# Eight places instead of five for layer 1's normalized rows, the neighbour weights moved to a later pool, and the first x tiles issued ahead of the convolution taps

## The chip, the cores and the metric

The kernel runs on one core of one Trainium2 chip. The metric is the device time of one execution in microseconds, and of several runs the median is compared. The engines are TensorE (PE in the profile; its weight loads are PEld), VectorE (DVE), ScalarE (ACT), GpSimd (POOL) and SyncE (SP), which here only issues DMAs.

## What is computed

The input x has 128 graphs of 128 nodes with 256 channels, and adj holds one 128x128 adjacency matrix for each graph. Two layers follow one another, each of them with a normalization in front and a residual around it:

```
h = relu(layernorm(x));  x = x + layer0(h, adj)
h = relu(layernorm(x));  x = x + layer1(h, adj)

layer0:  x_conv = relu(bn2(conv17(relu(bn1(conv1(h))))) + h)      # along the nodes
         s = h @ w_se.T + b_se;  A = exp(-|s_n - s_m|^2) * adj
         x_nmp = A @ relu(h @ w_msg.T + b_msg)
         result = GRU(input = [x_conv, x_nmp], state = h)
layer1:  the first 25 nodes, in five groups of 25, 9, 7, 6 and 6 of them:
         out_g = gcn(gcn(h_g, adj_g, W1[g], b1[g]), adj_g, W2[g], b2[g])
         fused = sum over g of softmax(fusion_w)[g] * out_g
```

All is in fp32. `gcn` normalizes the adjacency of its group by the degrees, multiplies by the weights and by the adjacency, and applies a ReLU.

## The kernel before

The 128 graphs form 32 groups of four (`q`), and the groups form two batches of 16 (`bat`). The convolution of width 17 is done through a small Fourier transform, so its weights are transformed once and then multiply the spectrum of the whole batch. For each batch there are two stages:

- `stage_a` (group by group): load x (`load_xa`, `load_x`, L362, on SP's queue, four tiles in its pool), layer normalization (`moments`, L271 to L274; `normalize`, L279), transposes with a ReLU (L389, L391), a store of the result to DRAM (`hTd`), the convolution of width 1 (L400, with `c1w`; L403, L405) and the forward transform (L411), which fills the spectrum `X`.
- `stage_b`: for each frequency, three products of the spectrum with the transformed taps (`wf`, loaded from the DRAM array `wfd`, L500), stored as `yd`.

Beside the first two stages runs a lane of other work: `tap_weights` (it transforms the taps, L453 and L458, and writes them to `wfd` through POOL's queue; in its middle it calls `load_late`), and then `early(q)` for each group, which loads `hT` and adj (L538, L540) and does the `neighbours` part: `pse` (L579), `ef` (L584, L587), the messages `pm` with `wmsg` (L599) and `msg` with `bmsg` (L602, L603), distances and adj (L611, L613), and the sum over neighbours (L624).

After both batches a last, long loop runs to the end of the program. In it are `stage_n` and `stage_c` for each group (the gates of the GRU: products at L706, gates at L719 to L807; then on POOL six operations for each group, L810 to L813; transposes back at L830, stores at L839) and layer 1:

- `setup_1` once;
- `rows(q)`: the layer normalization of the first 32 rows of each of a group's graphs: statistics (L904 to L906), a power on POOL (L907), then the normalized row `x1h` (L910 on VectorE, ReLU L911 on ScalarE);
- `prepare(blk)` for a block of four groups: degrees and normalized adjacency (L927 on POOL, L932 on VectorE, L938 and L943 on TensorE);
- `block(blk)`: products `py` of `x1h` with the adjacency (L989), copied into `yz` (L991, L992), two layers of weights (`first`, L1006 and L1008; `second`, L1015 and L1017), and the way back (L1037 to L1060), with the stores of the block on POOL's queue (L1069).

The order of the instructions is not the hardware's choice. Each stage is a Python generator, which yields the TensorE time that its step costs and the delay until its next step is due. The class `Order` keeps a clock of its own and picks, among lanes with weights, the step that is due and has had least of its share. Every engine then runs its own list in this order, and waits at an instruction until its operands are there and its place is free. So a delay in a `yield` and a condition in a `while` move instructions in the lists of all engines. `rows(q)` waits in this planner until `PY_DONE` holds row q − 5, since `x1h` has five places; block `blk` needs the rows 4·blk to 4·blk + 3, one for each group.

The start of the program issues, in this order: on ScalarE's queue the first constants and vectors; then the x tile of group 0 (SP), `c1w` (ScalarE), the x tile of group 1 (SP), the first taps `wt0` (five transfers, dealt to SP, POOL and ScalarE in turn) and the x tile of group 2 (SP). `fold()` then has the normalization of group 0 and the folding of the first batch norm into `c1w`.

## Time and profile before

| | |
|---|---|
| median of 9 runs | 2147.03 us (2141.74 to 2148.88) |
| profiled execution, its own time | 2141.94 us |
| its span, first to last instruction | 2140.1 us |
| granted clock of TensorE, mean | 0.983 |
| busy: TensorE, VectorE, ScalarE, POOL | 2071.3, 1152.7, 702.9, 719.3 us |
| bytes moved by DMA | 281.62 MB, mean 132 GB/s |

The stages lie in the span so: batch 0's `stage_a` until about 190 us and its `stage_b` from 206 to about 365; batch 1's until about 550 and 700; the last loop from there to 2140. Times in the span are counted from its start. In the lines of the profile the first number is the start, the second the busy time of what the line gathers, then come engine, line and operation, and in brackets the idle time of that engine just before, with what ended it.

### The profile page before, as it was taken

What the parts mean: (1) busy time and instruction counts of PE and PEld (TensorE: products, weight loads), DVE (VectorE), ACT (ScalarE), POOL (GpSimd) and SP (SyncE); (2) the same over time, 40 slices, a digit from 0 to 9 for tenths busy, and PEclk for the clock granted to TensorE, in tenths of its full rate; (3) what the DMA queues carried; (4) which work ended last, traced back from release to release, by engine and by line L of the source; (5) the groups of instructions that cost most, each with busy time, mean ns of one, the idle gap of its engine ahead of it and who ended that gap; (6) DMA issues with size and microseconds to landing.
All of it is one profiled execution on the core that took longest, in us unless ns stands there. A gap on an engine that the chain in (4) does not pass through costs nothing.

```text
span 2140.1 us, 30439 instructions
## 1 busy us (share of the span) xinstructions
PE 2071.3 (97%) x11124; PEld 1631.9 (76%) x11124; DVE 1152.7 (54%) x2711; ACT 702.9 (33%) x1545; POOL 719.3 (34%) x894
## 2 busy tenths in 40 slices
PE   6999999899999999999999999999999999999988
PEld 5667888788888777787678778868877787778765
DVE  5665444776444456545544554555555555644532
ACT  3564222344222243223223333233233323223223
POOL 2443665331565124303313233223223323232230
PEclk9999999999999999999999999999999999999999
DMA  8987878654787534222323223223232322323121
GB/s 180 277 259 238 274 261 263 190 168 138 242 260 255 164 94 139 73 77 72 87 60 111 66 80 101 71 77 81 83 89 69 94 89 72 83 73 101 36 67 50
DMA packets 186742, 281.62 MB, mean 132 GB/s; under 512 B 20637, under 2 KB 139938, under 8 KB 186594
## 3 DMA queue, kind: packets, MB, share of 16 engines
q1 hardware_dynamic: 155762, 184.81, 30.4%
q0 software_dynamic: 30000, 94.13, 13.7%
q8 instruction: 88, 1.44, 0.3%
q10 hardware_dynamic: 832, 0.74, 0.2%
q14 instruction: 60, 0.49, 0.1%
HBM read 187.34 MB, written 92.27 MB: 131 GB/s over the span
## 4 chain that ended last, share of the span: by engine, by line
PE 89%; DVE 3%; DMA 3%; POOL 2%; issue 1%; ACT 1%; SPq 0%; POOLq 0%; DVEq 0%; ACTq 0%
PE p L706 35%; PE pa L500 7%; PE pg L775 5%; PE ph L1006 5%; PE pz L1015 5%; PE pm L599 5%; PE pc L400 4%; PE pb L500 3%; PE pi L671 3%; PE pf L411 3%; PE px L624 3%; DMA wfd<-ws 2%; PE pg L1049 1%; PE po L830 1%; PE ph L389 1%
## 5 line engine op out<-in xcount | busy, mean ns | idle before, releaser
L810 POOL TENSOR_TENSOR d<-hTc,r 128x512 f32<-128x512 f32 x64 | 81.5, 1274 | 389.5 <-ACT r L807 389.4
L839 POOL DMA_DIRECT2D out<-xt x128 | 71.9, 567 | 250.0 <-DVE xt L836 245.7
L500 PE MATMUL pa<-wf,X 128*128 128x256 f32 x640 | 152.8, 382 | 0.0
L706 PE MATMUL p<-tc,wrz 128*128 128x256 f32 x512 | 132.3, 381 | 4.1 <-DVE tc L551 4.1
L706 PE MATMUL p<-th,wrz 128*128 128x256 f32 x512 | 132.6, 382 | 1.9 <-ACT u L737 1.9
L706 PE MATMUL p<-tm,wrz 128*128 128x256 f32 x512 | 132.3, 381 | 0.0
L500 PEld LDWEIGHTS pa<-wf,X 128*128 128x128 f32 x640 | 118.0, 190 | 17.2 <-issue 3.0
L523 DVE SCALAR_TENSOR_TENSOR y<-pa,kk 128x512 f32<-128x512 f32 x78 | 53.8, 690 | 140.5 <-ACT kk L522 140.3
L400 PE MATMUL pc<-c1w,hTa 128*128 128x256 f32 x512 | 124.7, 390 | 2.8 <-ACT ef L587 2.2
L719 ACT ACTIVATE r<-r,brz 128x256 f32<-128x256 f32 x128 | 58.1, 500 | 200.8 <-DVE r L752 172.9
L599 PE MATMUL pm<-wmsg,hT 128*128 128x256 f32 x512 | 122.3, 384 | 0.0
L775 PE MATMUL pg<-hTc,whn 128*128 128x512 f32 x256 | 120.9, 616 | 0.0
L1006 PE MATMUL ph<-yz,w 128*128 128x96 f32 (+3 forms) x640 | 114.4, 335 | 6.6 <-DVE yz L991 6.6
L1006 PEld LDWEIGHTS ph<-yz,w 128*128 128x128 f32 x640 | 92.0, 201 | 29.2 <-issue 16.5
L688 DVE SCALAR_TENSOR_TENSOR xc<-pc,s_bn,hTc 128x256 f32<-128x256 f32 x128 | 53.1, 477 | 110.6 <-PE pc L685 110.6
L400 PEld LDWEIGHTS pc<-c1w,hTa 128*128 128x128 f32 x512 | 96.2, 196 | 21.4 <-DVE h L403 4.0
L1008 ACT ACTIVATE hh<-ph,vec 128x96 f32<-128x96 f32 (+3 forms) x160 | 64.1, 402 | 147.4 <-PE ph L1006 138.3
L706 PEld LDWEIGHTS p<-tc,wrz 128*128 128x128 f32 x512 | 97.6, 191 | 18.2 <-DVE tc L551 4.9
L599 PEld LDWEIGHTS pm<-wmsg,hT 128*128 128x128 f32 x512 | 96.6, 191 | 15.3 <-issue 2.7
L706 PEld LDWEIGHTS p<-tm,wrz 128*128 128x128 f32 x512 | 97.9, 191 | 13.5
L1015 PE MATMUL pz<-hh,w 128*128 128x96 f32 (+3 forms) x640 | 107.5, 322 | 0.0
L706 PEld LDWEIGHTS p<-th,wrz 128*128 128x128 f32 x512 | 95.6, 191 | 14.1 <-ACT u L737 2.3
(197 smaller groups left out, 4470.1 us busy)
## 6 DMA issues: line engine op xcount, KB each, us to landing
wf<-wfd SPq DMA_DIRECT2D x160, 256.0 KB, 3.2
wfd<-ws POOLq DMA_DIRECT2D x64, 320.0 KB, 7.2
yd<-y POOLq DMA_DIRECT2D x80, 256.0 KB, 3.8
yt<-yd SPq DMA_DIRECT2D x64, 320.0 KB, 5.1
w<-in_W SPq DMA_DIRECT2D x40, 512.0 KB, 3.6
xa<-in_x SPq DMA_DIRECT2D x128, 128.0 KB, 4.9
hTd<-hTa POOLq DMA_DIRECT2D x32, 512.0 KB, 5.0
hT<-hTd SPq DMA_DIRECT2D x32, 512.0 KB, 4.5
```

What stands on the lines that cost most here:

```text
L400: nc.tensor.matmul(pc[:, i], hT[:, k, (2 * h + i) * N:(2 * h + i + 1) * N], c1w[:, k], start=(k == 0), stop=(k == 1))
L411: nc.tensor.matmul(pf[:, i, :F * NB], h1[:, 2 * h + i, k * P:(k + 1) * P], fwd, start=True, stop=True)
L500: nc.tensor.matmul(ps, xk(k), WF[f][:, k, s], start=(k == 0), stop=(k == 1))
L599: nc.tensor.matmul(pm[:, i], hT[:, k, j * N:(j + 1) * N], wmsg[:, k], start=(k == 0), stop=(k == 1))
L624: nc.tensor.matmul(px[:, dc, i], msgs[h][:, i, dc * P:(dc + 1) * P], aT[:, 2 * h + i], start=True, stop=True)
L671: nc.tensor.matmul(pi[b * 64:(b + 1) * 64], inv[:F], yt[:, b::2], start=True, stop=True)
L706: nc.tensor.matmul(ps[:, m], w[:, i, k, m * P:(m + 1) * P], factor(i, x, t), start=first and j == 0, stop=last and j == len(n) - 1)
L775: nc.tensor.matmul(pg, whn[:, k, dc * P:(dc + 1) * P], hT[:, k], start=(k == 0), stop=(k == 1))
L810: nc.gpsimd.tensor_sub(d, hT[:, dc], r[:, dc])
L839: nc.gpsimd.dma_start(out=out[q * GB + j, WIDE:].rearrange("(t n) c -> n t c", n=WIDE), in_=xt[j * WIDE:(j + 1) * WIDE, 1:4])
L1006: nc.tensor.matmul(ph, w1[:, k, m * P:(m + 1) * P], yz[:, k, :, o:o + n], start=(k == 0), stop=(k == 1))
L1015: nc.tensor.matmul(pz, w2[:, g, m, cc * P:(cc + 1) * P], hs[g][:, m], start=(m == 0), stop=(m == 3))
```

## The change

Four edits, each of a few lines:

1. `rows(q)` waits for `PY_DONE` of q − 8 in place of q − 5, `x1h` has eight places in place of five, and the delay between a row's statistics and its normalization is 4.0 in place of 2.5 in the planner's clock.
2. `wmsg` (2 KB of each partition) and `bmsg` (1 KB) are no longer tiles of the pools that live throughout; they are tiles of the pool `fr`, which is opened when `tap_weights` ends and closed when the neighbour part has been done for all groups. The three new places of `x1h` have 1 KB each.
3. So their loads (256 KB and 128 KB, on SP's queue) are issued at the end of `tap_weights`, after the pool is opened, and not in `load_late`.
4. At the start, `c1w` is issued on SP's queue after the x tiles of groups 0 and 1, and all five transfers of the first taps follow it on SP's queue; before, they were dealt to three queues.

In the changed file the lines from `load_late` up to the new loads stand four lines higher than before, and those from `stage_b` on where they stood or one or two lines further down.

```
-    wmsg = wp.tile([P, 2, D], FP, name="wmsg")
-    bmsg = cp.tile([P, D], FP, name="bmsg")
...
     def load_late():
         nc.sync.dma_start(out=wse, in_=w_se.rearrange("(k p) o -> p k o", p=P))
         nc.sync.dma_start(out=cst[:, CFIRST:], in_=consts[:, CFIRST:])
-        nc.sync.dma_start(out=wmsg, in_=w_msg.rearrange("(k p) o -> p k o", p=P))
-        nc.sync.dma_start(out=bmsg, in_=b_msg.partition_broadcast(P))
...
         LATE["fr"] = near.enter_context(tc.tile_pool(name="fr", bufs=1, reuse_waits="tile"))
+        LATE["wmsg"] = LATE["fr"].tile([P, 2, D], FP, name="wmsg")
+        LATE["bmsg"] = LATE["fr"].tile([P, D], FP, name="bmsg")
+        nc.sync.dma_start(out=LATE["wmsg"], in_=w_msg.rearrange("(k p) o -> p k o", p=P))
+        nc.sync.dma_start(out=LATE["bmsg"], in_=b_msg.partition_broadcast(P))
...
-                    nc.tensor.matmul(pm[:, i], hT[:, k, j * N:(j + 1) * N], wmsg[:, k],
+                    nc.tensor.matmul(pm[:, i], hT[:, k, j * N:(j + 1) * N], LATE["wmsg"][:, k],
...
-        while not (q in C_DONE and -1 in P_DONE and (q < 5 or q - 5 in PY_DONE)):
+        while not (q in C_DONE and -1 in P_DONE and (q < 8 or q - 8 in PY_DONE)):
...
-        yield 0.0, 2.5
-        x1h = S["x1h", q] = S["pool"].tile([P, D], FP, tag="x1h", name=f"x1h{q}", bufs=5)
+        yield 0.0, 4.0
+        x1h = S["x1h", q] = S["pool"].tile([P, D], FP, tag="x1h", name=f"x1h{q}", bufs=8)
...
     load_xa(0)
-    nc.scalar.dma_start(out=c1w, in_=conv1_w.rearrange("(k p) o -> p k o", p=P))
     load_xa(1)
-    load_taps(0, nc.sync, nc.gpsimd, nc.scalar)
+    nc.sync.dma_start(out=c1w, in_=conv1_w.rearrange("(k p) o -> p k o", p=P))
+    load_taps(0, nc.sync)
     load_xa(2)
```

## The prediction

> **What bounds the kernel now.** I read the page's engine line first, then the windows by stage, then the timeline at the places where TensorE stands still.

> ```profile
> PE 2071.3 (97%) x11124; PEld 1631.9 (76%) x11124; DVE 1152.7 (54%) x2711; ACT 702.9 (33%) x1545; POOL 719.3 (34%) x894
> ```

> TensorE is the bound. A change that takes no matmul away can win back only 2140.1 − 2071.3 = 69 us of idle, and what a throttled clock costs. The windows (span, PE, PEld, DVE, ACT, POOL busy, granted clock, DMA share, GB/s) tell where these lie:

> ```profile
> 0.00:50.00 50.00, 32.14 (x170) 24.81 (x171) 27.90 (x92) 16.35 (x33) 11.02 (x18) 0.97 0.87 180
> 150.00:200.00 50.00, 46.53 (x307) 34.90 (x306) 28.39 (x73) 25.90 (x59) 15.06 (x23) 1.00 0.77 240
> 700.00:1150.00 450.00, 434.71 (x2161) 335.44 (x2160) 236.03 (x557) 141.52 (x296) 122.71 (x150) 0.97 0.33 94
> 1150.00:2000.00 850.00, 850.00 (x4183) 659.57 (x4183) 464.57 (x1082) 264.48 (x561) 249.92 (x292) 1.00 0.30 83
> 2000.00:2050.00 50.00, 43.95 (x218) 31.33 (x214) 23.89 (x55) 14.70 (x30) 18.62 (x19) 0.98 0.08 20
> ```

> From 1150 to 2000 TensorE never stops, so three more places for normalized rows can gain nothing there. The 6.05 us missing in 2000–2050 are one wait. On the timeline:

> ```profile
> 2040.62 0.42 DVE L904 BATCH_NORM_STATS2 st<-x 128x6 f32<-128x256 f32 x1
> 2040.87 1.27 POOL L810 TENSOR_TENSOR d<-hTc,r 128x512 f32<-128x512 f32 x1 [18.57 <-ACT r L807]
> 2047.46 1.26 POOL L813 TENSOR_TENSOR z<-d,r 128x512 f32<-128x512 f32 x1
> 2048.68 1.08 POOL L907 TENSOR_TENSOR rs<-rs,cst 128x1 f32<-128x1 f32 x2
> 2049.28 0.41 DVE L910 TENSOR_SCALAR x1h<-x,mv,rs 128x256 f32<-128x256 f32 x1 [5.63 <-POOL rs L907]
> 2049.61 0.37 DVE L991 COPY yz<-py 128x212 f32<-128x212 f32 x1
> 2050.04 8.13 PE L1006 MATMUL ph<-yz,w 128*128 128x400 f32 x16 [6.09 <-DVE yz L991]
> ```

> Read it backwards. TensorE waits for a copy of 0.37 us (L991). This stands in VectorE's queue behind L910 of a row that TensorE does not need yet, and L910 waits for POOL's power (L907), which stands behind the six operations of group 31's gate (L810 to L813). The row's statistics (L904) came only at 2040.62, since `rows` waits until `PY_DONE` holds the row five back; 0.25 us later POOL began the gate.

> [...]

> ```profile
> 2036.00:2040.00 4.00, 4.00 (x23) 2.81 (x21) 3.15 (x8) 0.80 (x2) 0.00 (x0) 1.00 0.00 0
> 2050.00:2054.00 4.00, 3.96 (x6) 2.17 (x7) 0.44 (x1) 1.40 (x4) 3.03 (x6) 0.50 0.57 119
> 2054.00:2058.00 4.00, 4.00 (x11) 2.06 (x10) 0.00 (x0) 1.19 (x2) 1.88 (x7) 0.87 0.06 12
> 2058.00:2062.00 4.00, 4.00 (x29) 3.55 (x28) 3.20 (x11) 2.11 (x5) 1.72 (x4) 1.00 0.55 158
> ```

> The loss is 3.96×0.50 + 4.00×0.13 = 2.5 us; the same 16 matmuls of L1006 took 8.13 us here and 5.59 us at 1900.60, again 2.5. Shorter stalls are less regular: after 1.75 us at 118.7 the clock was 0.50, after 1.91 us at 1048.7 it stayed at 1.00. [...]

> **The change part by part**, against the profiled execution (2141.94 us, span 2140.1). It is 5.1 below the median of the runs shown (2147.03), so I carry the sum over to the median.

> *Eight places, end of the program.* Rows 29 and 30 no longer wait for products of block 6. In the new instruction order POOL's two L907 stand ahead of group 31's gate, where POOL was idle for 18.57 us, which hides them (2 × 0.54 us); L910 stands ahead of the block's copies. Then L991 follows its own product: L989 ends at 2043.95, the copy takes 0.38, so L1006 starts about 2044.4 in place of 2050.04: −5.7 us, and −2.5 us of clock. What is late next: `po` of group 31 (L830), which TensorE would reach near 2050, 8.2 earlier than 2058.01, while POOL ends the gate at 2048.7 (with the powers in front at most 1.1 later): at worst just in time. The edges of block 7 (L927) precede their matmul by over 5 us. **−8.2.** Bounds: −5 (clock stays low or `po` waits) to −9.

> *Eight places, earlier blocks.* The new order also moves POOL's L1069 stores of block 0, three issues (1.64 us) that at 1038.45 stood before a gate and delayed it; its end let TensorE idle 1.91 us at 1048.67. They now come after: −2.0. But POOL's L927 (2.44 us) of block 2 moves behind a store and a power, and its five reductions on VectorE (L932, 1.26 us) now stand in front of a copy L777 and the row's L910; `py` of block 1 then waits about 2.8 us where it waited 0.94: +1.9. The clock after it was already low (0.52 in 1065–1070), so I add nothing. At 883 (3.13 us, clock 0.7 after it) L910 moves behind two gate operations while its product moves later too: −0.4; at 926 and 1101, 0.2 later each: +0.4. Together **−0.1**, bounds −4 (no waits left) to +4 (a second throttled stretch of 2.5). The pause of 4.0 instead of 2.5 in `rows` only shapes this order.

> *x in front of the taps.* Group 0's tile lands earlier: its first reader began at 11.46 after 4.77 us of waiting, with six transfers of the taps and `c1w` under way beside it. But the second group's matmuls are held by VectorE, whose queue has the statistics of group 2 ahead of them:

> ```profile
> 22.74 0.43 DVE L271 BATCH_NORM_STATS2 st<-xa 128x6 f32<-128x256 f32 x1 [2.18 <-DMA xa<-in_x]
> ```

> and the third tile has the same 3.09 MB in front of it in both kernels (512 + 512 + 256 KB + 1088 KB of taps + itself 512 + 212 KB on ScalarE's queue). TensorE starts up to 5 us sooner and waits longer at 23–26. **0**; bounds −3 (DMA better used) to +1.7 (one queue at 156 KB/us, as in 12–20 us, in place of 177 with three).

> *Neighbour weights in the late pool.* 384 KB leave the loads at 72–74 us, a stage with DMA share 1.00: at some 279 KB/us 1.4 us, of which I count **−0.5**, since later x tiles are still queued. The same 384 KB now stand on SP's queue in front of group 0's hT (L538) and adj (L540), and the first waits for the tap writes that land at 175.36. hT left at 171.46; now about 176.3, landing 183–185 where L579 asks at 182.46. About 1–2 us, of which the 1.23 us wait at 187.98, set by the last tap write, takes back a part: **+1.2**; bounds 0 to +6.

> Sum: −8.2 − 0.1 + 0 − 0.5 + 1.2 = **−7.6 us**: 2134.3 against the profiled execution, **2139.4** against the median. 0.2%, about what a measurement can tell, is 4.3 us.

> **Rivals.**
> - *Gain at the end, and the start gains too.* For it: the long DMA wait at 11.46. Against: the same bytes before tile 2. With −3 at the start and −1.4 in the middle: 2135.5.
> - *Moved waits eat most.* For it: the wait at 1062, now longer, can throttle once more (+2.5), and `po` behind the gate can keep the end's gain at −5.7. Net −2.6: 2144.4.
> - *Slower: the late weights hold up group 0's neighbours.* POOL's tap writes bring 2.38 of the 4.34 MB moved in 174–190. If they keep their share, hT lands near 190.5: 8 us of idle less 1.4 absorbed, two throttled stretches (5), adj behind it (1), and the spectrum's first weights, issued from 190.14, 768 KB later (3): 15.6 in place of 1.2, so 2153.8. It decides once the delay costs over 8.8 us, that is with hT landing after about 188. Against it: [...]hT is only 896 KB away from the head of its own.
> - *No effect at the end*: excluded by the instruction order, unless another wait stands there.

> **How the numbers follow.** Forecast 0.52, start gains too 0.13, most eaten 0.20, slower 0.15. The forecast's own range is 2136.5 to 2143. For 8 in 10 I take 2134 to 2149: it leaves out the slower case and little else. Faster by over 0.2% (below 2142.7): nine tenths of the forecast, all of the second, a little of the third: 0.63. Slower (above 2151.3): 0.12. Within: 0.25.

> **What would show it.** Right: no idle over 1 us before L1006 near 2040–2044 and clock 1.00 after it; L907 before L810 of group 31; L1069 of block 0 after the gate; a wait of 2–3 us at `py` near 1062; L538's first landing at 183–185. Wrong: an idle of 3 us or more before L830 or L1006 at the end, TensorE over 4 us idle at 182–190, or the second group's matmuls starting before 24 us or after 28.

## The result, and the profile after

| | before | changed |
|---|---|---|
| median of the runs | 2146.62 us (33 runs) | 2137.42 us (11 runs, 2131.39 to 2139.71) |
| ratio | | 0.9959, interval 0.995 to 0.9967 |
| profiled execution, its span | 2141.94, 2140.1 us | 2140.55, 2138.8 us |

The change takes 9.2 us away; 7.6 had been forecast. The two profiled executions differ by only 1.4 us, and they can't be compared by their spans: the one of before is among the fastest of its kernel, the other is slower than all timed runs of its own. They have to be compared stage by stage. The windows of the changed kernel by stage, the columns as in the prediction:

```profile
0.00:50.00 50.00, 31.87 (x163) 24.71 (x164) 26.69 (x89) 15.23 (x30) 9.64 (x16) 0.90 0.88 174
150.00:200.00 50.00, 46.58 (x310) 34.90 (x303) 29.76 (x80) 26.83 (x60) 16.61 (x24) 1.00 0.75 236
700.00:1150.00 450.00, 434.59 (x2160) 335.49 (x2159) 237.15 (x556) 142.23 (x300) 124.02 (x151) 0.97 0.34 97
1150.00:2000.00 850.00, 850.00 (x4172) 661.21 (x4171) 464.38 (x1078) 263.19 (x558) 252.50 (x296) 0.99 0.30 83
2000.00:2050.00 50.00, 50.00 (x246) 35.86 (x244) 28.61 (x63) 16.51 (x33) 11.07 (x12) 1.00 0.09 20
2050.00:2100.00 50.00, 49.05 (x295) 35.19 (x295) 19.29 (x50) 16.57 (x38) 19.00 (x30) 1.00 0.29 82
```

The last row in the kernel before:

```profile
2050.00:2100.00 50.00, 49.49 (x279) 35.70 (x280) 17.91 (x47) 15.72 (x37) 11.96 (x24) 0.92 0.29 82
```

The gain stands in the last two rows: in 2000–2050 TensorE is busy for all 50 us (43.95 before), and in 2050–2100 its clock is 1.00 in place of 0.92. Two clocks have become worse: 0.90 in place of 0.97 in the first 50 us, and 0.99 in place of 1.00 in 1150–2000, where TensorE is as full as before. Both are told below. The timeline at the end of the program, POOL first, then VectorE's copy and TensorE:

```profile
2033.76 0.56 POOL L908 TENSOR_TENSOR rs<-rs,cst 128x1 f32<-128x1 f32 x1 [3.00 <-DVE rs L907]
2049.30 1.27 POOL L811 TENSOR_TENSOR d<-hTc,r 128x512 f32<-128x512 f32 x1 [14.99 <-ACT r L808]
2052.43 0.38 DVE L992 COPY yz<-py 128x212 f32<-128x212 f32 x1 [0.34 <-PE py L990]
2052.86 5.69 PE L1007 MATMUL ph<-yz,w 128*128 128x400 f32 x16 [0.47 <-DVE yz L992]
2058.39 1.03 PE L831 MATMUL po<-cst,z 128*128 128x128 f32 x8
```

The later of the two powers (L907 before, L908 now) runs 15.5 us ahead of the last group's gate, not behind it; the other one runs at 1998.41. The copy waits only for its own product, TensorE for 0.47 us, and the 16 matmuls take 5.69 us in place of 8.13. The transposes of group 31 (L831) follow without a wait.

A way to compare the two traces whatever their start: take the same instruction in both and subtract. These shifts (us, against the trace of before) are worked out so, from the starts of three tiles that ScalarE writes (`kk` in `stage_b`, `u` in the gates, `zt` on a block's way back), for the changed kernel and three experiments told below:

| place (time in before) | changed | e1 | e4 | e7 |
|---|---|---|---|---|
| end of batch 1's `stage_b` (686) | +5.2 | +2.0 | +5.1 | +3.2 |
| group 9's gate (1141) | +3.4 | −0.1 | +3.5 | +2.9 |
| group 31's gate (2013) | +8.4 | +5.0 | +5.1 | +2.9 |
| last block's way back (2124) | −1.3 | −4.7 | −4.6 | −6.8 |

The last step, from group 31's gate to the last way back, is −9.7 us in all four, and in e8, e9, e10 and e12 too. What lies before it differs, even where the program is the same: the edit of e4 bears on the last rows alone, and its trace stands 5.1 us behind at 686.

### The profile page after: what moved, and what is told of

Its sections match the earlier page's. It is cut to its first block, busy times and chain, and to the rows that moved or that the text cites. A ratio compares the mean times of both kernels' runs of the same rounds, so it can differ in the third digit from the quotient of the medians.

```text
span 2138.8 us, 30436 instructions
## 1 busy us (share of the span) xinstructions
PE 2072.8 (97%) x11124; PEld 1634.9 (76%) x11124; DVE 1158.6 (54%) x2711; ACT 702.6 (33%) x1545; POOL 719.1 (34%) x893
## 4 chain that ended last, share of the span: by engine, by line
PE 89%; DVE 3%; DMA 3%; POOL 2%; issue 2%; ACT 1%; SPq 0%; POOLq 0%; DVEq 0%; ACTq 0%
PE p L707 35%; PE pa L500 7%; PE pg L776 5%; PE ph L1007 5%; PE pm L599 5%; PE pz L1016 5%; PE pc L396 4%; PE pb L500 3%; PE pi L672 3%; PE pf L407 3%; PE px L625 3%; DMA wfd<-ws 2%; PE pg L1050 1%; PE po L831 1%; PE pc L686 1%
## 5 line engine op out<-in xcount | busy, mean ns | idle before, releaser
L599 PE MATMUL pm<-wmsg,hT 128*128 128x256 f32 x512 | 122.6, 384 | 0.0
L599 PEld LDWEIGHTS pm<-wmsg,hT 128*128 128x128 f32 x512 | 96.8, 192 | 15.4 <-issue 2.7
```

The lines of the kernel that those rows point to most:

```text
L599: nc.tensor.matmul(pm[:, i], hT[:, k, j * N:(j + 1) * N], LATE["wmsg"][:, k], start=(k == 0), stop=(k == 1))
```

## The experiments

**e1: the first edit alone**, on the kernel before; there is room for eight places without moving the weights.

```
-        while not (q in C_DONE and -1 in P_DONE and (q < 5 or q - 5 in PY_DONE)):
+        while not (q in C_DONE and -1 in P_DONE and (q < 8 or q - 8 in PY_DONE)):
...
-        yield 0.0, 2.5
-        x1h = S["x1h", q] = S["pool"].tile([P, D], FP, tag="x1h", name=f"x1h{q}", bufs=5)
+        yield 0.0, 4.0
+        x1h = S["x1h", q] = S["pool"].tile([P, D], FP, tag="x1h", name=f"x1h{q}", bufs=8)
```

> The kernel before with the first edit alone: eight places, a wait for the row eight back, a delay of 4.0. Theory (all of the gain comes from the last wait, 6 us of idle and 2.5 us of throttled clock): 7 to 10 us faster than before, the profile without the wait near 2050, and the first 700 us as before. Rival (the loads of the first two stages give a share): 3 to 6 us faster.

Measured: 2136.8 against 2145.61, ratio 0.9952 (0.994 to 0.9964). All of the gain that can be measured is here.

**e2: the start alone**, `c1w` and all first taps on SP's queue.

> The kernel before with the new order of the first loads alone: c1w behind the x tiles of groups 0 and 1, all first taps on SP's queue. Theory (the third tile has the same bytes in front of it): within 1.5 us of before, TensorE begins about 5 us sooner and then stands still that much longer ahead of the second group's transposes. Rival (the early start is kept): 3 to 5 us faster.

Measured: 2145.2 against 2145.61, ratio 0.9994 (0.9986 to 1.0002). No change. The first reader of each x tile on VectorE in this run (groups 0, 1 and 2):

```profile
6.50 0.43 DVE L271 BATCH_NORM_STATS2 st<-xa 128x6 f32<-128x256 f32 x1 [0.92 <-DMA xa<-in_x]
...
13.18 0.41 DVE L271 BATCH_NORM_STATS2 st<-xa 128x6 f32<-128x256 f32 x1
...
24.14 0.43 DVE L271 BATCH_NORM_STATS2 st<-xa 128x6 f32<-128x256 f32 x1 [8.55 <-DMA xa<-in_x]
```

Groups 0 and 1 are read 5 us sooner (11.46 and 18.14 before), group 2 at 24.14 where it was 22.74, and the statistics of group 2 stand in VectorE's queue ahead of what TensorE needs for group 1. In the changed kernel group 2 is read at 23.15. TensorE then waits longer for the second group than it did (9.0 us here, 8.2 in the changed kernel, 2.8 before), and its clock in the first 50 us is lower (0.90 in both, 0.97 before): the loss is 3.2 us of its busy time in the changed kernel and 1.7 in the trace of before.

**e3: the late weights alone.**

> The kernel before with wmsg and bmsg in the late pool alone. Theory: -0.5 us at 72 to 120, +1.2 at 182 to 190, together within 1.5 us of before, and hT of group 0 issued near 176 in place of 171.5. Rival (the late weights hold up group 0's neighbours): 3 us slower or more.

Measured: 2147.18 against 2145.61, ratio 1.0003 (0.999 to 1.0016). Nothing that can be measured. The trace shows the wait that was forecast, somewhat longer:

```profile
178.62 0.68 SPq L538 DMA_DIRECT2D hT<-hTd  x1
```

```profile
187.95 1.08 PE L579 MATMUL pse<-hT,wse 128*32 128x128 f32 x16 [3.35 <-DMA hT<-hTd]
```

Group 0's hT is issued at 178.62 behind the two weights (in e1, without them, at 170.11), and TensorE waits 3.35 us for it. The wait also costs clock in this trace (0.71 in 185–190 and 0.60 in 190–195): 16 matmuls of `pm` (L599) right after it take 6.18 us, where they took 3.72 before. In the changed kernel's trace the wait is 2.09 us, those matmuls again take 3.72, and the later wait for `lr` (1.23 us at 187.98 before) is gone.

**e4: the power's place without the places.** Five places as before, but rows 29 and 30 wait for the row five back only after their power:

```
-        while not (q in C_DONE and -1 in P_DONE and (q < 5 or q - 5 in PY_DONE)):
+        while not (q in C_DONE and -1 in P_DONE and (q < 5 or q in (29, 30) or q - 5 in PY_DONE)):
...
         nc.gpsimd.tensor_tensor(rs, rs, c("mhalf")[:, :1], ALU.pow)
         yield 0.0, 2.5
+        while q in (29, 30) and q - 5 not in PY_DONE:
+            yield 0.0, 0.5
```

> The kernel before, five places, with one difference: rows 29 and 30 take their statistics and their power on POOL without waiting for the row five back, and only the normalized row waits for its place; so both powers stand ahead of the last gates in POOL's queue. Theory (the loss is the power's place in POOL's queue, not the missing place): 6 to 9 us faster than before, no wait over 1 us near 2045. Rival (the row's place itself is what is waited for): 0 to 3 us faster, with the wait now on the place.

Measured: 2137.31 against 2145.61, ratio 0.9961 (0.9948 to 0.9974): the gain of the full change, with no place added. POOL and TensorE at the end of this run:

```profile
2032.26 0.56 POOL L907 TENSOR_TENSOR rs<-rs,cst 128x1 f32<-128x1 f32 x1 [4.87 <-DVE rs L906]
2045.94 1.29 POOL L810 TENSOR_TENSOR d<-hTc,r 128x512 f32<-128x512 f32 x1 [13.12 <-ACT r L807]
```

```profile
2049.50 5.69 PE L1008 MATMUL ph<-yz,w 128*128 128x400 f32 x16 [0.47 <-DVE yz L993]
```

So the cause was two powers of 0.54 us behind 7.8 us of other work in POOL's queue (their statistics on VectorE moved ahead with them). The missing place only put them there, through the planner's wait.

**e5 and e11: what the throttled clock costs.** Into the wait of the kernel before go matmuls that nobody needs, ahead of block 6's first L1006; the wait itself stays. The edit of e5 has 12 of them; in e11 `range(12)` is `range(6)`.

```
+            if (blk, g) == (6, 0):
+                warm = pgat.tile([P, 2, D], FP, tag="gat", name="warm")
+                for i in range(12):
+                    nc.tensor.matmul(warm.rearrange("p a c -> p (a c)"), ident,
+                                     S["w1", blk * NG][:, 0], start=True, stop=True)
```

> The kernel before, with twelve matmuls of 128x512 that nobody needs put in TensorE's queue just ahead of block 6's first L1006, in the wait near 2045 (12 x 0.43 = 5.1 us, so they end before the wait does). The wait itself stays. Theory (the idle costs 2.5 us of halved clock on top of its length): 2 to 3 us faster than before although work is added, and a granted clock of 1.00 right after the wait. Rival (the 8.13 us of L1006 have another reason, such as its operands): no change, within 0.5 us.

> The kernel before with half the filler (six matmuls, each of two passes of 0.43 us: 5.2 us), so that it ends before the wait does. Theory: clock 1.00 after the wait, L1006 takes 5.6 us in place of 8.1, 2 to 4.5 us faster than before. Rival (the filler only moves the low clock): within 1 us of before.

e5: 2144.78 against 2145.93, ratio 1.0 (0.9992 to 1.0008). The size was wrong: each of these calls is two matmul instructions in the trace (24 for 12), so the filler took 10.46 us, not 5.1, and ran past the wait. Still no loss can be measured. e11, with the size that was meant: 2141.65 against 2145.76, ratio 0.9985 (0.9975 to 0.9996). A kernel with 5.3 us of useless work added is about 3 us faster (by the interval 1 to 5). Its trace:

```profile
2050.24 5.31 PE L1003 MATMUL warm<-w,cst 128*128 128x512 f32 x12
```

```profile
2058.00:2062.00 4.00, 4.00 (x13) 2.17 (x12) 0.00 (x0) 1.78 (x3) 3.68 (x9) 1.00 0.48 101
...
2070.00:2074.00 4.00, 4.00 (x33) 3.59 (x32) 2.31 (x7) 1.08 (x3) 0.04 (x1) 1.00 0.00 0
```

The clock stays at 1.00, right after the wait and also further on. By the shifts, e11 gains 4.05 us between group 31's gate and the last way back. In the trace of before the windows of 5 us give 2.48 us lost in 2050–2055 and 0.65 + 1.05 in 2065–2075: 4.18. So the last step of −9.7 is, to within 0.1, the idle time before L1006, from 6.09 to 0.47 us (5.6), and the clock (4.2).

**e6: where the half clock in the full stretch comes from.** The changed kernel, with the 16 small matmuls of `pa` (L939, in `prepare`; 25 of 128 rows, 64 columns) cut into four pieces that the planner puts between other products; the price of the step that holds the rest is lowered.

```
                              c("et")[:NN, :RP], start=True, stop=True)
+            if p in (1, 3, 5):
+                yield 0.25, 0.6
...
-        yield 2.0, 7.0
+        yield 0.5, 7.0
```

> The changed kernel, with the 16 small matmuls of pa (25x64) of each block cut into four pieces that the planner puts between other products; same work. Theory (the half clock seen once per block in the stretch without idle comes from these 2 us with few rows at work): the stretches at 0.5 near 1323, 1525, 1726 and 1927 and the longer one after 1070 go, 5 to 8 us faster than the changed kernel, so 14 to 17 faster than before. Rival (the throttle comes by itself, about every 200 us): as the changed kernel, 8 to 10 us faster than before, with as many such stretches.

The changed kernel, TensorE at the `pa` of one block, and then the windows around it (the clock is the third column from the end):

```profile
1320.23 1.99 PE L939 MATMUL pa<-cst,b 25*128 25x64 f32 x16
1322.07 0.40 PE L944 MATMUL pdg<-dg,cst 25*128 25x80 f32 x2
...
1323.51 3.42 PE L1007 MATMUL ph<-yz,w 128*128 128x112 f32 x16
```

```profile
1320.00:1323.00 3.00, 3.00 (x23) 2.64 (x22) 1.63 (x5) 0.00 (x0) 0.00 (x0) 1.00 0.00 0
1323.00:1327.00 4.00, 4.00 (x21) 3.86 (x20) 1.08 (x5) 1.09 (x4) 2.06 (x3) 0.57 0.00 0
```

TensorE has no gap here (busy for 4.00 of 4.00 us) and yet falls to half clock for 3.4 us (1.7 lost), right after 2.2 us in which only 25 rows worked. In e6 no such stretch is left between 1150 and 2000, where the changed kernel has four; its line:

```profile
1150.00:2000.00 850.00, 850.00 (x4163) 656.40 (x4161) 466.56 (x1085) 263.87 (x561) 251.31 (x296) 1.00 0.30 82
```

With the count of traces in the last section that settles the cause, but it brings no gain: 2138.76 against 2145.93, ratio 0.9968 (0.9955 to 0.998), no faster than the changed kernel. Some of it went into the seams: by the distances of starts, the steps into, within and out of `pa` cost 3.4 us above the usual in 1150–2000, where the changed kernel has 0.4 going in. And two waits of 1.9 us each end at 1052.76 and 1056.69, where the changed kernel has one of 2.8 that ends at 1069. The rest is open.

**e7: the changed kernel with the delay of 2.5.**

> The changed kernel with the delay of 2.5 in place of 4.0 between statistics and normalized row. Theory (the places and the wait for the row eight back make the gain, the delay only shapes the order): within 2 us of the changed kernel, 7 to 11 us faster than before. Rival (the longer delay is what puts the powers ahead of the gates): the wait near 2045 is back, within 2 us of before.

Measured: 2136.09 against 2145.93, ratio 0.9959 (0.9945 to 0.9974), as the changed kernel. Its trace keeps the order of before until the end: the shift against before stays at 2.9 from 1141 to 2013, where the changed kernel goes from 3.4 to 8.4. The medians don't show this difference.

**e8 to e12: the third tile.** Its x tile goes ahead of the first taps.

```
     load_xa(1)
     nc.sync.dma_start(out=c1w, in_=conv1_w.rearrange("(k p) o -> p k o", p=P))
-    load_taps(0, nc.sync)
     load_xa(2)
+    load_taps(0, nc.sync)
```

> The changed kernel with the x tile of group 2 issued ahead of the first taps too (behind c1w). Theory (the second group's transposes wait for the statistics of group 2, whose tile has 1088 KB of taps ahead of it): the wait of 8.3 us at 18.4 goes down to under 3, TensorE is 4 to 6 us ahead at the third group; of this 0 to 4 us are left at the end of the stage, which the DMAs bound. Rival (another tile is what is waited for): the wait stays over 6 us, no change.

Measured: 2130.87 against 2145.93, ratio 0.9936 (0.9922 to 0.9951), which just touches the interval of the changed kernel (0.995 to 0.9967). TensorE in the changed kernel, then in e8:

```profile
13.56 4.85 PE L396 MATMUL pc<-c1w,hTa 128*128 128x256 f32 x16
26.60 2.25 PE L385 MATMUL ph<-cst,xa 128*128 128x128 f32 x8 [8.18 <-issue]
```

```profile
13.45 4.70 PE L396 MATMUL pc<-c1w,hTa 128*128 128x256 f32 x16
18.82 1.69 PE L385 MATMUL ph<-cst,xa 128*128 128x128 f32 x8 [0.67 <-PE pc L396]
```

The wait of 8.2 us is 0.67, the clock stays at 1.00 through the first 50 us, and of the 8.9 us won by the third group's start (+1.2 against before in the changed kernel, −7.7 in e8) about 7 are left at 686 (+5.2 against −1.9). By the ratios the gain over the changed kernel is about 5 us.

> The changed kernel with both: the third tile ahead of the taps and the delay of 2.5. Theory (the shorter delay leaves out the three extra stretches of half clock, 5 us, and brings back a wait of 2 us near 1050): 2 to 4 us faster than the third tile alone, 17 to 19 faster than before. Rival (the throttled stretches are a matter of phase, not of the order): as the third tile alone, 14 to 16 faster.

e9: 2128.58 against 2145.76, ratio 0.9928 (0.9908 to 0.9947). Its trace has two stretches of half clock in 1150–2000, e8's has four; the medians of the two can't be told apart. The interval of e9 lies wholly below that of the changed kernel.

> The same, but wmsg and bmsg stay in the pools and among the loads of the kernel before (there is room for eight places beside them). Theory (the late weights cost hT of group 0 about 3 us at 180 and give 0 to 1.4 at 75): 0 to 3 us faster than with the late weights. Rival (384 KB less in the crowded stretch is worth more): 1 to 3 us slower.

e10, which has the delay of 2.5 of e9: 2130.01 against 2145.76, ratio 0.9926 (0.9903 to 0.9949). Late or early weights make no difference that can be measured.

> The kernel before with the eight places (delay 2.5) and the third tile ahead of the taps, but with the queues of before: c1w and part of the taps on ScalarE's and POOL's queues, early weights. Theory (what counts at the start is that 1088 KB of taps no longer stand before the third tile[...]): 1 to 4 us slower than with one queue, 12 to 16 us faster than before. Rival (the one queue counts, not the order): the start as before, 9 to 10 us faster than before.

e12: 2130.89 against 2145.48, ratio 0.9937 (0.9924 to 0.9951). TensorE starts at 15.12 again, as before, and is only 2.4 us ahead of before at the third group (e8: 7.7), but the ratio can't be told from that of e10, the same kernel with one queue. So the order of the tiles is what pays; that one queue pays too is not shown.

## Why the prediction was right, step by step

- *The wait at the end* (−8.2, measured −9.7 in eight traces): right in its mechanism, shown by e1 and e4. The rival that a place is needed falls with e4. The term was mis-sized by the clock: I counted one stretch at half clock (2.5), and there were two. The second, of 1.7 us in 2065–2075, follows `pa` of the last block (L938 at 2066.30). It is there in the three traces that keep the wait (before, e2, e3), and in e5, e11 and all traces without the wait it is gone; the last section tells what goes with that. `po` behind the gate was in time, as forecast: no wait at L831.
- *The earlier blocks* (−0.1): the waits came as forecast: the 2 us near 1049 are gone, `py` of block 1 waits 2.83 us (forecast 2.8), the wait near 885 is 0.6 shorter (forecast 0.4), the two small ones are 0.3 longer each (forecast 0.2). In sum TensorE's idle time in 686–1141 is 0.1 us longer than before. (Two waits of the prediction are shorter on the trace's own lines: 0.77 us for `py` where it has 0.94, 1.59 at 118.7 where it has 1.75.) What the forecast lacked: from 686 to 2013 the changed kernel loses 3.2 us, and two more stretches at half clock account for 3.4 (6.8 us lost in 1150–2000 against 3.4). The shifts at 1141 say nothing more than that: 16 matmuls of `pz`, about 1.7 us, stand behind group 9's gate in the changed kernel and ahead of it before, so that it seems to gain 1.8 up to there and to lose 5.1 behind. I had written that nothing can be gained where TensorE never stops; it didn't occur to me that something can be lost.
- *x ahead of the taps* (0): right, and e2 bears out the bytes ahead of the third tile as the reason; that those on ScalarE's queue count like those on SP's was my estimate. The third tile came 0.4 to 1.4 us later, inside the bound of 1.7. The term lacked the clock here too: the longer wait costs 1.5 us of it in the changed kernel's trace.
- *The late weights* (+0.7 together): e3 holds nothing that can be measured. TensorE's wait for hT was 2.1 to 3.4 us, above the 1 to 2 of the forecast, and the later wait took part of it back.
- *The rival of a slower kernel* decided with hT landing after about 188. TensorE had it at 187.9 in the changed kernel's trace, which itself ran 3.3 us behind there, so at 184.6 in the time of the trace of before; the delay cost 2 us, not 8.8.
- *The medians*: the sum was made against a trace and carried to the median. That held because the last step is the same in every trace that lacks the wait, not because traces repeat: the part ahead of it moves by 5 us from run to run. The measured ratio stands for 7 to 11 us, so it tests the term of the end and none of the small ones. That 7.6 came so near 9.2 is in part luck: at the end 1.5 us of gain were missing from the sum, and in the changed kernel's trace 3.4 us of loss in 1150–2000.

## What to carry to other kernels

A short operation on an engine that is mostly idle can stop the busiest engine if it is queued behind long work (here two powers of 0.54 us behind 7.8 us, on an engine busy for 34% of the span); look for who stands ahead of it in its queue before adding buffers, since moving its condition (e4) can do what more buffers do. Price a wait of TensorE with the clock that follows it (here 4.2 us on top of 5.6 us of idle time). And when loads are put in order at the start, count the bytes ahead of the last tile that gates the flow, not of the first (e8: 1088 KB of taps behind the third tile instead of ahead of it, about 5 us).

## What was not expected of the hardware

By these records, whether half clock follows a `pa` goes with its place on the grid. In 1150–2000 the 13 traces that don't spread it have 52 of them, each 2.2 us long with the two matmuls of `pdg` behind it. Half clock follows 34. Every one of these lies between two lines of the grid, to 0.03 us. Of the other 18, 16 cross a line, and two come within 0.06 us of one. In the trace of before, the `pa` at 1314.20 crosses a line 0.14 us after its start, and the clock stays:

```profile
1315.00:1320.00 5.00, 5.00 (x38) 4.71 (x38) 2.17 (x7) 1.41 (x4) 2.02 (x3) 1.00 0.00 0
```

The last block's `pa`, where it is whole, crosses a line too in e5, in e11 and in the traces without the wait, and no half clock follows it. The three traces with a delay of 4.0 and `pa` whole (changed, e1, e8) have four such stretches each in 1150–2000, the ten with 2.5 have one to three; whether the order of the instructions brings this about is not shown.

With a wait the records show the same. One wait of 3.15 us, which ends at 724.3 in the trace of before and at 724.5 in e12's:

```profile
720.00:725.00 5.00, 1.85 (x16) 1.44 (x16) 3.88 (x12) 1.52 (x6) 0.00 (x0) 0.88 0.94 245
725.00:730.00 5.00, 4.80 (x15) 1.92 (x14) 0.69 (x1) 0.60 (x1) 0.00 (x0) 0.50 0.10 30
730.00:735.00 5.00, 5.00 (x19) 3.98 (x18) 0.44 (x2) 0.60 (x1) 0.00 (x0) 0.59 0.96 214
```

```profile
720.00:725.00 5.00, 1.85 (x18) 1.19 (x17) 4.01 (x13) 1.76 (x6) 0.00 (x0) 1.00 0.80 249
725.00:730.00 5.00, 5.00 (x30) 3.24 (x29) 0.80 (x3) 1.19 (x2) 0.00 (x0) 1.00 0.46 111
730.00:735.00 5.00, 5.00 (x27) 4.43 (x26) 1.62 (x4) 1.99 (x5) 0.00 (x0) 1.00 1.10 241
```

The idle time is equal (TensorE busy 1.85 of 5 us); the first lost 4.7 us of clock to it, the other none. In the trace of before 2.7 us of this wait lie between two lines of the grid. In e12's a line splits it into 1.63 and 1.51 us, and it is the only one of the 14 traces with less than 1.67 us of this wait between two lines, and the only one whose clock stays. Whether this wait of 3.15 us costs clock is thus in part a matter of chance here. It goes with the scatter of the runs: the traces of e10 and e12, the fastest of all, have 11 stretches of half clock, those of the other kernels with `pa` whole 13 to 18. Over the whole trace of before the throttle costs 32 us, summed in windows of 5 us as TensorE's busy time by what the clock lacks to 1.00. That is nearly half as much as its 69 us of idle time, and it stands in no list of waits.
